# Layer 1 of a four-layer graph network: a node tile's transform made in two parts, the tile's own rows apart from its neighbours' sums

## The chip, the cores and the metric

The kernel runs on one core of one Trainium2 chip. The metric is the device time of one execution in microseconds (us), smaller is better. A core has five engines that run side by side, each in its own order: PE (TensorE, matrix products; its weight loads are shown as PEld), DVE (VectorE), ACT (ScalarE), POOL (GpSimd) and SP (SyncE, which only issues transfers), and 16 DMA engines that move data between the chip's memory (DRAM in the code) and the on-chip memories SBUF and PSUM. PE writes only to PSUM. A PSUM bank holds 128 rows of 512 numbers.

## What is computed

`x` is 6250 nodes of 256 numbers, `src` and `dst` name the ends of 100,000 edges, sorted by `dst`. The reference, cut:

```python
h = jnp.maximum(_layernorm(x, axis=-1), 0.0)
# in _L0_gnn_ref, features = h:
deg = jax.ops.segment_sum(jnp.ones(edge_dst.shape[0]), edge_dst, num_segments=n)
h = _sage_mean(features, edge_src, edge_dst, n, deg, W1_self, W1_neigh, b1)
h = _sage_pool(h, edge_src, edge_dst, n, deg, W2_pool, b2_pool, W2_self, W2_neigh, b2)
h = _sage_gcn(h, edge_src, edge_dst, n, deg, W3_neigh, b3)
h = _sage_mean(h, edge_src, edge_dst, n, deg, W4_self, W4_neigh, b4)
return x + (h @ W_fc + b_fc)

def _sage_mean(h, src, dst, n, deg, W_self, W_neigh, b):
    msum = jax.ops.segment_sum(h[src], dst, num_segments=n)
    h_neigh = msum / jnp.clip(deg, 1.0)[:, None]
    return h @ W_self + h_neigh @ W_neigh + b

def _sage_pool(h, src, dst, n, deg, W_pool, b_pool, W_self, W_neigh, b):
    hp = jax.nn.relu(h @ W_pool + b_pool)
    hmax = jax.ops.segment_max(hp[src], dst, num_segments=n)
    hmax = jnp.where(deg[:, None] > 0, hmax, 0.0)
    return h @ W_self + hmax @ W_neigh + b
```

The end nodes are not spread evenly: `dst` is 6250 times the square of a uniform number, so low nodes have many edges and high ones few.

## The kernel before, in words

Nodes lie in 49 tiles of 128 rows. Edges lie in 782 tiles of 128, in groups of four (G = 4). The first 8 node tiles of layer 1 are "hubs" (H1): for them a dense matrix of edge counts is built and multiplied. The other 41 tiles get their sums by gathers.

Layer 1 produces for each node tile the row that layer 2's pooling needs, `relu(h1 @ W_pool + b_pool)`, where h1 is layer 1's result. Because no nonlinearity stands between, `W1_self @ W2_pool` and `W1_neigh @ W2_pool` are multiplied out beforehand into `Wa` and `Wb`, and the biases into `crow`. So a tile's row is relu(own rows @ `Wa` + mean of the neighbours @ `Wb` + `crow`). It is stored in the DRAM table `tab_p`, from which layer 2 gathers. The transposed own rows and means are stored in `tab_t`, which layer 2 loads again.

The loop of layer 1 is `sums` (line 355), 474 steps of one edge tile each:

- `gather(j)`: POOL issues an indirect DMA of 128 rows of `tab_h` into one of 14 slots of `ring` (L374). A slot comes free when PE has used it.
- `one_hot(j)`: DVE makes the matrix `hot` that sorts the edges to rows (L370).
- PE multiplies `hot` with the three parts of the gathered rows (high, middle and low bits) into the bank `pg` (L392), 3 matmuls a step.
- `hub.advance`: some of the hubs' work. A build is two ACT instructions (`ht` L298, `hs` L300), one of DVE (`hm` L302) and a matmul into `pb` (L308), with a copy to `A` (L312) now and then; a product is three matmuls into `pd` (L430). All builds of the first hub are listed ahead of the loop.
- `next(todo[0])`: one piece of the oldest node tile that is ready. `todo` is a queue of generators; each call runs to the next `yield`.

After every fourth step DVE adds `pg` into the sums `acc` of the tiles that this group can touch (L409, L411), and a tile whose last group this is goes to `todo` as `done1(d, acc)`. Hubs go there when their dense product ends.

`done1` has, before the change, four pieces: (1) degree, its reciprocal (L787 to L789) and the mean `m1` on ACT (L791); (2) on PE six matmuls with the identity that transpose the three parts of the own rows `Z1` and add them up (L797) and two transposes of `m1` (L800), all into one bank `pt_m`, a copy by ACT to `th` (L802) and its store to `tab_t` (L803); (3) the product with `Wa` into `pm_hp` (L807); (4) the product with `Wb` onto it (L810), the addition of `crow` by DVE (L813), Relu by ACT (L814) and the store to `tab_p` (L815). An f32 product with 512 columns stands in the trace as two records for each matmul. The pools `pst` (tag `pt`) and `psm` (tag `pm`) have one bank each here.

The order in which each engine runs its instructions is not the order of the code: a scheduler goes by the code's order as a priority, and by its own estimate of when operands and buffers are ready. What it fixed is called the compiled order below. At run time each engine keeps to its order and waits on semaphores. SP issues nearly all plain transfers of this stage, in its own fixed order.

Layer 2 begins with gathers from `tab_p` (L1111), and each needs all of that table, so none starts before the last store of layer 1.

Of the kernel before, what the change touches and what calls it, by code (L numbers as in the profile page):

```python
# [9 lines left out]
F32 = mybir.dt.float32  # L10
# [4 lines left out]
AF = mybir.ActivationFunctionType  # L15
# [5 lines left out]
P = 128  # L21
# [51 lines left out]
def fast_path(  # L73
# [15 lines left out]
    nc = tc.nc  # L89
    N, FI = x.shape  # L90
    E = src.shape[0]
    FH = W1_self.shape[1]
    FO = W_fc.shape[1]
    NT = (N + P - 1) // P
    NFULL = N // P
    NREM = N - NFULL * P
    NP = NT * P
    T = (E + P - 1) // P
    EP = T * P
    KI = FI // P  # L100
# [9 lines left out]
    for d in range(NT):  # L110
        m, s = _edges_below(d * P, E, N)
        m1, s1 = _edges_below((d + 1) * P, E, N)
# [3 lines left out]
    JC = g_of[HUB[0]][0] * G // P  # L116
# [5 lines left out]
    for d in range(NT):  # L122
        m, s = _edges_below(d * P, E, N)
        m1, s1 = _edges_below((d + 1) * P, E, N)
# [7 lines left out]
    H1, H3, H4 = HUB  # L132
# [7 lines left out]
    for w0, w1_ in ((0, WT * H1), (WT * H1, NW)):  # L140
        for k in range(k_of[w0]):
            n = sum(1 for w in range(w0, w1_) if k_of[w] > k)
# [9 lines left out]
    dram = ctx.enter_context(tc.tile_pool(name="fdram", bufs=1, space=DRAM))  # L152

    tab_h = dram.tile([NP, 3 * FI], BF16, name="tab_h")
    tab_t = dram.tile([NT, P, FH], F32, name="tab_t")
    tab_p = dram.tile([NP, FH], F32, name="tab_p")
    tab_r = dram.tile([NP, 3 * FH], BF16, name="tab_r")
    tab_s = dram.tile([NP, 3 * FO], BF16, name="tab_s")
    tab_a = dram.tile([H4, P, NT, P // 2], BF16, name="tab_a")
# [27 lines left out]
    ident = const.tile([P, P], F32, name="identf")  # L187
    make_identity(nc, ident)
    ident_b = const.tile([P, P], BF16, name="ident_b")
# [30 lines left out]
    def bank(pool, tag, name, shape=None, bufs=None):  # L220
        t = pool.tile([P, FH], F32, tag=tag, name=name, **({"bufs": bufs} if bufs else {}))
        if shape is None:
            return t
        n = math.prod(shape)
        if len(shape) == 1:
            return t[:, :n]
        return t[:, :n].rearrange("p (a b) -> p a b", b=shape[1])
# [124 lines left out]
                self.done += 1  # L352


    def sums(pool, psg, table, F, srcT, keyT, jb, h, done, deep, hub, wait=0, counts=0, todo=()):

        ring = pool.tile([P, deep, 3 * F + 2 * counts], BF16, name="ring", bufs=1)  # L360
        if counts:
            nc.gpsimd.memset(ring[:, :, 3 * F :], 1.0)
        acc = {}
        ahead = 6
        hot = {}
        j0 = g_of[h][0] * G

        def one_hot(j):
            hot[j] = pool.tile([P, P], BF16, name="hot", bufs=ahead + 4)
            nc.vector.tensor_scalar(hot[j], iota_b, keyT[:, j - jb : j - jb + 1], None,  # L370
                                    op0=ALU.is_equal)

        def gather(j):
            nc.gpsimd.indirect_dma_start(  # L374
                out=ring[:, j % deep, : 3 * F], out_offset=None, in_=table,
                in_offset=bass.IndirectOffsetOnAxis(ap=srcT[:, j - jb : j - jb + 1], axis=0),
            )

        for j in range(j0, j0 + ahead):
            one_hot(j)  # L380
        for g in range(g_of[h][0], NG):
            pg = bank(psg, "pg", "pg", (F + counts,))
            n = min(G, T - g * G)
            for k in range(n):
                j = g * G + k
                X = ring[:, j % deep, :]
                gather(j)
                if j + ahead < T:
                    one_hot(j + ahead)
                for part in (2, 0, 1):  # L390
                    c = counts if part == 2 else 0
                    nc.tensor.matmul(  # L392
                        pg[:, : F + c], hot[j], X[:, part * F : (part + 1) * F + c],
                        start=(k == 0 and part == 2), stop=(k == n - 1 and part == 1),
                    )
                del hot[j]
                at = j - j0 + 1
                if at > wait:
                    hub.advance(math.ceil(len(hub.work) * (at - wait) / (T - j0 - wait)))
                if todo and next(todo[0], None) is None:  # L400
                    todo.pop(0)
            for d in range(h, NT):
                g0, g1 = g_of[d]
                if not g0 <= g <= g1:
                    continue
                m = M[:, m_at[d] + g - g0 : m_at[d] + g - g0 + 1]
                if d not in acc:
                    acc[d] = pool.tile([P, F + counts], F32, name="acc", bufs=3)
                    nc.vector.tensor_scalar(acc[d], pg, m, None, op0=ALU.mult)  # L409
                else:  # L410
                    nc.vector.scalar_tensor_tensor(acc[d], pg, m, acc[d],  # L411
                                                   op0=ALU.mult, op1=ALU.add)
                if g == g1:
                    todo.append(done(d, acc.pop(d)))
        while todo:
            for _ in todo.pop(0):
                pass
# [66 lines left out]
    Z1 = zpool.tile([P, NT, 3 * FI + 2], BF16, name="Z1")  # L484
# [8 lines left out]
    Wa = w1pool.tile([P, KI, FH], F32, name="Wa")  # L493
    Wb = w1pool.tile([P, KI, FH], F32, name="Wb")
    crow = w1pool.tile([P, FH], F32, name="crow")
    srcT = w1pool.tile([P, (JR - JC) * P], I32, name="srcT")
    keyT = w1pool.tile([P, (JR - JC) * P], F32, name="keyT")
# [4 lines left out]
    with ExitStack() as pro:  # L502
# [104 lines left out]
        i = 0  # L607
# [166 lines left out]
    with ExitStack() as on:  # L774
        pst = on.enter_context(tc.tile_pool(name="pst1", bufs=1, space=PSUM))
        psm = on.enter_context(tc.tile_pool(name="psm1", bufs=1, space=PSUM))
        psg = on.enter_context(tc.tile_pool(name="psg1", bufs=2, space=PSUM))
        psb = on.enter_context(tc.tile_pool(name="psb1", bufs=2, space=PSUM))
        psd = on.enter_context(tc.tile_pool(name="psd1", bufs=2, space=PSUM))
        wk = on.enter_context(tc.tile_pool(name="fl1", bufs=2))  # L780

        def h0_row(s):
            return Z1[:, s, :]

        def done1(d, acc):
            r = rmean[:, d : d + 1]
            nc.vector.tensor_copy(deg[:, d : d + 1], acc[:, FI : FI + 1])  # L787
            nc.vector.tensor_scalar_max(r, acc[:, FI : FI + 1], 1.0)
            nc.vector.reciprocal(r, r)  # L789
            m1 = wk.tile([P, FI], F32, name="m1")  # L790
            nc.scalar.activation(m1, acc[:, :FI], AF.Copy, scale=r)  # L791
            yield 1
            pt = bank(pst, "pt", "pt_m", (2 * KI, P))
            for k in range(KI):
                for part in range(3):
                    c = part * FI + k * P
                    nc.tensor.matmul(pt[:, k, :], Z1[:, d, c : c + P], ident_b,  # L797
                                     start=(part == 0), stop=(part == 2))
            for k in range(KI):
                nc.tensor.transpose(pt[:, KI + k, :], m1[:, k * P : (k + 1) * P], ident)  # L800
            th = wk.tile([P, 2 * KI, P], F32, name="th")
            nc.scalar.copy(th, pt)  # L802
            nc.sync.dma_start(tab_t[d].rearrange("p (k n) -> p k n", n=P), th)  # L803
            yield 1
            ph = bank(psm, "pm", "pm_hp")
            for k in range(KI):
                nc.tensor.matmul(ph, th[:, k, :], Wa[:, k, :], start=(k == 0), stop=False)  # L807
            yield 1
            for k in range(KI):
                nc.tensor.matmul(ph, th[:, KI + k, :], Wb[:, k, :], start=False,  # L810
                                 stop=(k == KI - 1))
            hp = wk.tile([P, FH], F32, name="hpf")
            nc.vector.tensor_add(hp, ph, crow)  # L813
            nc.scalar.activation(hp, hp, AF.Relu)  # L814
            nc.sync.dma_start(tab_p[d * P : (d + 1) * P, :], hp)  # L815

        As = [wk.tile([P, NT, P], F8, name=f"A{i}", bufs=1) for i in range(2)]
        keys = (sk1, mk1, 0)
        todo = []
        builds = [build(d, As[d % 2], keys, wk, psb) for d in range(H1)]  # L820
        denses = [dense(range(NT), lambda s, A=As[d % 2]: A[:, s, :], h0_row, FI, psd,
                        lambda acc, d=d: todo.append(done1(d, acc)), extra=1)
                  for d in range(H1)]
        work = list(builds[0])
        first = len(work)
        for d in range(H1):
            work += merged(denses[d], builds[d + 1]) if d + 1 < H1 else denses[d]
        hub = Hub(work)
        hub.advance(first)
        todo.append(segments())  # L830
        sums(wk, psg, tab_h, FI, srcT, keyT, JC * P, H1, done1, 14, hub, counts=1, todo=todo)
    layer1.close()


# [62 lines left out]
    jb = g_of[H3][0] * G  # L897
# [1029 lines left out]
```

## Time and profile before

| | |
|---|---|
| median of 18 runs | 3542.53 us (3525.9 to 3566.07) |
| the profiled execution | 3548.44 us |
| its span, first to last instruction | 3546.6 us |
| mean granted clock of PE | 0.872 of full speed |
| busy share PE, DVE, ACT, POOL | 73%, 55%, 25%, 58% |
| layer 1's loop, first gather to first gather of `tab_p` | 148.7 to 1055.4 us |

The span in 40 equal slices, as the page shows it, each digit tenths of a slice:

```profile
PE   2457777778876745676676767679689889688887
...
POOL 5363555455437676677766765550366666566663
PEclk9767888889898877788897888889899999899999
DMA  6443454445449999999999999991699999766664
```

Layer 1 is about slices 2 to 12. Layer 2, slices 13 to 28, is the stretch in which the DMA engines are full. Then come layers 3 and 4.

The columns of a group of instructions are: line, engine, operation, what it writes and reads, count, then busy time in us and mean ns of one, then the engine's idle time just before them and what ended it. A row of windows gives, for a stretch A:B in us, its length, each engine's busy time with its number of instructions, the granted clock, the share of the DMA engines and GB/s. A wait is put down to what came last by the profile.

### The profile page before, as it was taken

What the parts mean: (1) busy time and instruction counts of PE and PEld (TensorE: products, weight loads), DVE (VectorE), ACT (ScalarE), POOL (GpSimd) and SP (SyncE); (2) the same over time, 40 slices, a digit from 0 to 9 for tenths busy, and PEclk for the clock granted to TensorE, in tenths of its full rate; (3) what the DMA queues carried; (4) which work ended last, traced back from release to release, by engine and by line L of the source; (5) the groups of instructions that cost most, each with busy time, mean ns of one, the idle gap of its engine ahead of it and who ended that gap; (6) DMA issues with size and microseconds to landing.
All of it is one profiled execution on the core that took longest, in us unless ns stands there. A gap on an engine that the chain in (4) does not pass through costs nothing. (4 is left out here: it accounts for less than half of the span.)

```text
span 3546.6 us, 41171 instructions
## 1 busy us (share of the span) xinstructions
PE 2597.7 (73%) x12699; PEld 1437.3 (41%) x12699; DVE 1953.6 (55%) x5075; ACT 903.4 (25%) x2383; POOL 2040.6 (58%) x2260
## 2 busy tenths in 40 slices
PE   2457777778876745676676767679689889688887
PEld 1134444455544322232232323234233333477776
DVE  4744444444426767665665655553266566466664
ACT  2556555444414556621111111100000001000000
POOL 5363555455437676677766765550366666566663
PEclk9767888889898877788897888889899999899999
DMA  6443454445449999999999999991699999766664
GB/s 188 147 127 111 143 151 140 142 149 155 145 145 396 365 353 367 352 389 376 376 337 335 381 364 323 332 319 53 254 331 363 360 360 336 242 187 188 187 193 139
DMA packets 403406, 913.34 MB, mean 258 GB/s; under 512 B 58064, under 2 KB 151202, under 8 KB 403144
## 3 DMA queue, kind: packets, MB, share of 16 engines
q0 software_dynamic: 146560, 514.74, 44.1%
q1 hardware_dynamic: 198532, 340.44, 25.8%
q10 hardware_dynamic: 58084, 55.44, 5.0%
q8 instruction: 103, 1.69, 0.2%
q14 instruction: 127, 1.04, 0.1%
HBM read 610.65 MB, written 300.55 MB: 257 GB/s over the span
## 5 line engine op out<-in xcount | busy, mean ns | idle before, releaser
L1111 POOL DMA_INDIRECT X<-tab_p,srcIf x782 | 825.6, 1056 | 421.5 <-issue 204.5
L392 PE MATMUL pg<-ring,hot 128*128 128x256 bf16 (+2 forms) x3390 | 699.1, 315 | 131.4 <-DMA ring<-tab_r,srcE 51.5
L374 POOL DMA_INDIRECT ring<-tab_h,srcT x474 | 451.3, 952 | 427.0 <-PE pg L392 164.7
L430 PE MATMUL pd<-zt,ac 128*128 128x256 bf16 (+1 forms) x3462 | 581.5, 300 | 56.7 <-issue 41.3
L430 PE MATMUL pd<-r,ae 128*128 128x512 bf16 x1536 | 413.8, 421 | 211.6 <-DVE acc L908 100.0
L392 PEld LDWEIGHTS <-hot 128*128 128x128 bf16 x3390 | 336.9, 101 | 391.7 <-issue 222.4
L374 POOL DMA_INDIRECT ring<-tab_r,srcE x342 | 333.4, 975 | 190.4 <-PE pg L392 74.5
L1116 DVE SCALAR_TENSOR_TENSOR X<-X,samef,X 128x512 f32<-128x512 f32 x385 | 289.0, 751 | 270.3 <-DMA X<-tab_p,srcIf 137.2
L430 PEld LDWEIGHTS <-ac 128*128 128x128 fp8e4 x3462 | 337.9, 98 | 205.0 <-issue 78.7
L411 DVE SCALAR_TENSOR_TENSOR acc<-pg,M,acc 128x257 f32<-128x257 f32 (+2 forms) x518 | 274.5, 560 | 248.1 <-PE pg L392 204.3
L374 POOL DMA_INDIRECT ring<-tab_s,srcE x314 | 298.8, 952 | 190.8 <-issue 66.3
L308 PE MATMUL pb<-hm,hs 128*128 128x392 bf16 x781 | 266.0, 389 | 160.5 <-ACT A L312 36.1
L300 ACT ACTIVATE hs<-ht,onef 128x128 bf16<-128x128 bf16 x781 | 291.0, 395 | 361.4 <-PE pb L308 198.6
L1116 DVE SCALAR_TENSOR_TENSOR X<-X,samef 128x512 f32<-128x512 f32 x391 | 293.3, 751 | 145.0 <-DMA X<-tab_p,srcIf 113.0
L430 PEld LDWEIGHTS <-ae 128*128 128x128 fp8e4 x1536 | 162.7, 106 | 470.9 <-issue 346.6
L370 DVE TENSOR_SCALAR hot<-iota_bf,keyE 128x128 bf16<-128x128 bf16 x656 | 154.0, 268 | 166.7 <-PE pg L392 107.7
L1050 PE MATMUL pm_prf<-unf,hTf 128*128 128x512 f32 x392 | 208.3, 658 | 30.8 <-ACT hTf L1041 18.2
L302 DVE TENSOR_SCALAR hm<-iota_w,mk 128x392 bf16<-128x392 f16 x461 | 155.3, 345 | 133.4 <-PE pb L308 65.0
L370 DVE TENSOR_SCALAR hot<-iota_bf,keyT 128x128 bf16<-128x128 bf16 x474 | 126.2, 277 | 150.8 <-PE pb L308 55.4
L312 ACT ACTIVATE A<-pb 128x392 fp8e4<-128x392 f32 x288 | 140.2, 491 | 262.3 <-PE pb L308 134.0
L430 PE MATMUL pd<-Z,A 128*128 128x256 bf16 (+1 forms) x1176 | 197.5, 283 | 2.4 <-issue 1.7
L1183 DVE TENSOR_SCALAR_CACHE_REDUCE many<-ac 128x896 bf16<-128x896 fp8e4 (+2 forms) x144 | 139.0, 965 | 88.7 <-DMA ac<-tab_a 69.2
(273 smaller groups left out, 2805.6 us busy)
## 6 DMA issues: line engine op xcount, KB each, us to landing
runb<-X SPq DMA_DIRECT2D x391, 512.0 KB
tab_r<-r SPq DMA_DIRECT2D x49, 384.0 KB
tab_a<-A SPq DMA_DIRECT2D x18, 784.0 KB
tab_t<-th SPq DMA_DIRECT2D x49, 256.0 KB
tab_p<-hpf SPq DMA_DIRECT2D x49, 256.0 KB
th<-tab_t ACTq DMA_DIRECT2D x49, 256.0 KB
X<-tab_p,srcIf POOLq DMA_INDIRECT x782
ac<-tab_a ACTq DMA_DIRECT2D x108, 112.0 KB
```

What stands on the lines that cost most here:

```text
L300: nc.scalar.activation(hots[0], t, AF.Relu, bias=one, scale=-1.0)
L302: nc.vector.tensor_scalar(hots[1], iota_w, mk[:, r : r + 1], None, op0=ALU.is_equal)
L308: nc.tensor.matmul(hold[0], hots[0], hots[1], start=(k == 0), stop=(k == k_of[w] - 1))
L312: nc.scalar.copy(A[:, :, c : c + WIN], hold[0].rearrange("p (s c) -> p s c", c=WIN), saturate=True)
L370: nc.vector.tensor_scalar(hot[j], iota_b, keyT[:, j - jb : j - jb + 1], None, op0=ALU.is_equal)
L374: nc.gpsimd.indirect_dma_start(out=ring[:, j % deep, : 3 * F], out_offset=None, in_=table, in_offset=bass.IndirectOffsetOnAxis(ap=srcT[:, ...
L392: nc.tensor.matmul(pg[:, : F + c], hot[j], X[:, part * F : (part + 1) * F + c], start=(k == 0 and part == 2), stop=(k == n - 1 and part == 1),
L411: nc.vector.scalar_tensor_tensor(acc[d], pg, m, acc[d], op0=ALU.mult, op1=ALU.add)
L430: nc.tensor.matmul(hold[0][:, : F + c], a, z[:, part * F : (part + 1) * F + c], start=(s == ss[0] and part == 2), stop=(s == ss[-1] and pa ...
L1050: nc.tensor.matmul(pm, hT[:, c, :], un[:, c, :], start=False, stop=(c == KH - 1))
L1111: nc.gpsimd.indirect_dma_start(out=X[:, k, :], out_offset=None, in_=tab_p, in_offset=bass.IndirectOffsetOnAxis(ap=srcI[:, t : t + 1], axis=0),
L1116: nc.vector.scalar_tensor_tensor(X[:, k, :], prev, same[:, t : t + 1], X[:, k, :], op0=ALU.mult, op1=ALU.max,)
```

## The change

The node tile's transform becomes two generators. `own1(d)` transposes the own rows, stores them to `tab_t`, three steps later multiplies them with `Wa`, adds `crow` and stores the f32 row to a new DRAM table `tab_g`. The loop takes one piece of it in every step, through a new argument `beside`, from its first step on: the tiles 8 to 48 in order, and after each third of them a hub. `done1` loads the row from `tab_g` in its first piece, transposes only `m1` three steps later, multiplies with `Wb` three steps after that, and adds the loaded row in place of `crow`. It has seven pieces in place of four. `own1` uses the same two banks, and `tab_t` of a tile is written by two transfers.

```diff
+    tab_g = dram.tile([NP, FH], F32, name="tab_g")
...
-    def sums(pool, psg, table, F, srcT, keyT, jb, h, done, deep, hub, wait=0, counts=0, todo=()):
+    def sums(pool, psg, table, F, srcT, keyT, jb, h, done, deep, hub, wait=0, counts=0, todo=(),
+             beside=iter(())):
...
+                next(beside, None)
                 if todo and next(todo[0], None) is None:
                     todo.pop(0)
...
+        def own1(d):
+            pt = bank(pst, "pt", "pt_h", (KI, P))
+            for k in range(KI):
+                for part in range(3):
+                    c = part * FI + k * P
+                    nc.tensor.matmul(pt[:, k, :], Z1[:, d, c : c + P], ident_b,
+                                     start=(part == 0), stop=(part == 2))
+            hT = wk.tile([P, KI, P], F32, name="h0T")
+            nc.scalar.copy(hT, pt)
+            nc.sync.dma_start(tab_t[d, :, : KI * P].rearrange("p (k n) -> p k n", n=P), hT)
+            yield 1
+            yield 1
+            yield 1
+            pm = bank(psm, "pm", "pm_g")
+            for k in range(KI):
+                nc.tensor.matmul(pm, hT[:, k, :], Wa[:, k, :], start=(k == 0),
+                                 stop=(k == KI - 1))
+            g = wk.tile([P, FH], F32, name="grow")
+            nc.vector.tensor_add(g, pm, crow)
+            nc.sync.dma_start(tab_g[d * P : (d + 1) * P, :], g)
+            yield 1
...
         def done1(d, acc):
...
             nc.scalar.activation(m1, acc[:, :FI], AF.Copy, scale=r)
+            g = wk.tile([P, FH], F32, name="grow2")
+            nc.sync.dma_start(g, tab_g[d * P : (d + 1) * P, :])
             yield 1
-            pt = bank(pst, "pt", "pt_m", (2 * KI, P))
+            yield 1
+            yield 1
+            pt = bank(pst, "pt", "pt_m", (KI, P))
             for k in range(KI):
-                for part in range(3):
-                    c = part * FI + k * P
-                    nc.tensor.matmul(pt[:, k, :], Z1[:, d, c : c + P], ident_b,
-                                     start=(part == 0), stop=(part == 2))
-            for k in range(KI):
-                nc.tensor.transpose(pt[:, KI + k, :], m1[:, k * P : (k + 1) * P], ident)
-            th = wk.tile([P, 2 * KI, P], F32, name="th")
+                nc.tensor.transpose(pt[:, k, :], m1[:, k * P : (k + 1) * P], ident)
+            th = wk.tile([P, KI, P], F32, name="th")
             nc.scalar.copy(th, pt)
-            nc.sync.dma_start(tab_t[d].rearrange("p (k n) -> p k n", n=P), th)
+            nc.sync.dma_start(tab_t[d, :, KI * P :].rearrange("p (k n) -> p k n", n=P), th)
+            yield 1
+            yield 1
             yield 1
             ph = bank(psm, "pm", "pm_hp")
             for k in range(KI):
-                nc.tensor.matmul(ph, th[:, k, :], Wa[:, k, :], start=(k == 0), stop=False)
-            yield 1
-            for k in range(KI):
-                nc.tensor.matmul(ph, th[:, KI + k, :], Wb[:, k, :], start=False,
+                nc.tensor.matmul(ph, th[:, k, :], Wb[:, k, :], start=(k == 0),
                                  stop=(k == KI - 1))
-            hp = wk.tile([P, FH], F32, name="hpf")
-            nc.vector.tensor_add(hp, ph, crow)
-            nc.scalar.activation(hp, hp, AF.Relu)
-            nc.sync.dma_start(tab_p[d * P : (d + 1) * P, :], hp)
+            nc.vector.tensor_add(g, ph, g)
+            nc.scalar.activation(g, g, AF.Relu)
+            nc.sync.dma_start(tab_p[d * P : (d + 1) * P, :], g)
...
+        def owns():
+            hubs = list(range(H1))
+            for i, d in enumerate(range(H1, NT)):
+                yield from own1(d)
+                if i % 3 == 2 and hubs:
+                    yield from own1(hubs.pop(0))
+            for d in hubs:
+                yield from own1(d)
...
-        sums(wk, psg, tab_h, FI, srcT, keyT, JC * P, H1, done1, 14, hub, counts=1, todo=todo)
+        sums(wk, psg, tab_h, FI, srcT, keyT, JC * P, H1, done1, 14, hub, counts=1, todo=todo, beside=owns())
```

## The prediction

> **What bounds the kernel now.** The change touches layer 1 alone; in the compiled order of the changed kernel every engine's instructions from the first gather of `tab_p` on stand as before. So I read layer 1: first the waits of PE between 160 and 1060 us, then the stretches, one tile close up, and the gathers.
>
> The waits of PE (line, waited for: us in total, times, longest):
>
> ```profile
> PE pt_m L800 <- ACT m L791: 43.7, 14, 7.6
> PE pm_hp L807 <- ACT th L802: 39.4, 23, 3.8
> PE pt_m L800 <- issue: 20.8, 11, 3.2
> ...
> PE pt_m L800 <- ACT hs L300: 14.1, 4, 6.4
> ```
>
> All rows of `pt_m` L800 and `pm_hp` L807 together are 143 us: in a node tile PE stands before the transposes of `m1`, and again before the product, one step after the copy to `th`. One such tile, in order of time (start, length, engine, line):
>
> ```profile
> 612.84 0.57 PE L797 MATMUL pt_m<-ident_b,Z 128*128 128x128 bf16 x6
> ...
> 613.82 0.87 DVE L411 SCALAR_TENSOR_TENSOR acc<-pg,M,acc 128x257 f32<-128x257 f32 x2
> ...
> 616.32 0.49 ACT L791 ACTIVATE m<-acc,rmeanf 128x256 f32<-128x256 f32 x1
> ...
> 616.86 0.53 PE L800 MATMUL pt_m<-identf,m 128*128 128x128 f32 x2 [3.23 <-ACT m L791]
> ```
>
> The same stretch as windows (length, PE, PEld, DVE, ACT, POOL busy, granted clock, DMA share, GB/s):
>
> ```profile
> 604.80:613.60 8.80, 8.80 (x76) 6.80 (x73) 5.07 (x16) 4.62 (x13) 5.15 (x6) 1.00 0.57 167
> 613.60:616.80 3.20, 0.03 (x1) 0.00 (x0) 2.45 (x12) 3.10 (x9) 2.46 (x3) 1.00 0.39 111
> 616.80:623.90 7.10, 5.12 (x14) 2.65 (x15) 1.09 (x6) 1.87 (x5) 2.84 (x3) 0.52 0.50 153
> ```
>
> An idle of 3.2 us is followed by 7.1 us at half clock, so a stall costs about 3.2 + 3.4 us. Layer 1 in six stretches, same columns; the cuts are the first matmuls of steps 64, 90 and 196 (counted by the three `ring` matmuls of a step) and the end of step 473:
>
> ```profile
> 148.50:248.90 100.40, 50.15 (x253) 30.25 (x254) 40.35 (x157) 41.06 (x133) 67.35 (x71) 0.69 0.48 136
> 248.90:294.30 45.40, 27.57 (x75) 8.03 (x73) 22.07 (x72) 39.79 (x131) 7.13 (x8) 0.53 0.17 54
> 294.30:334.20 39.90, 29.64 (x159) 18.30 (x158) 14.71 (x55) 14.89 (x42) 22.91 (x24) 0.88 0.52 157
> 334.20:521.20 187.00, 142.19 (x821) 91.64 (x820) 85.07 (x301) 96.12 (x263) 101.03 (x106) 0.84 0.48 140
> 521.20:1038.50 517.30, 424.03 (x2481) 272.32 (x2479) 216.83 (x769) 228.74 (x581) 252.85 (x266) 0.88 0.49 147
> 1038.50:1055.40 16.90, 9.63 (x41) 4.62 (x38) 2.92 (x24) 3.82 (x7) 0.01 (x1) 0.96 0.35 122
> ```
>
> I call them Start, Block (the builds of the first hub, without gathers), S, B, C and Tail. In C a step takes 517.3 / 277 = 1.87 us and every other engine is under half busy: PE's work, its stalls and the half clock behind them set the pace. POOL waits for ring slots that PE frees late:
>
> ```profile
> POOL ring L374 <- PE pg L392: 164.7, 85, 35.5
> POOL ring L374 <- PE pb L308: 124.4, 89, 4.7
> ```
>
> A gather that waits for nothing takes 0.95 us and a 0.30 us gap, 1.255 in all; in Start, where PE is idle half the time, POOL makes 71 in 100.4 us, 1.41 each. That is the next bound.
>
> **PE's work at full clock.** A 256-column matmul costs 0.109 us (nine `pd` in 0.98 us on the chain of waits); a `pb` of 392 columns 0.167 by columns. From the last tile's timeline (L807 at 1047.39, L810 at 1049.21; L797 at 1045.22, L800 at 1045.55): one half of the product 1.82 or 1.72 us (four records), six Z transposes 0.33, the pair of `m1` 0.24 to 0.34. A tile is 4.1 us today; its own part (Z transposes and `Wa`) 2.1, its neighbours' part 2.0. Work in S: 78 `pg`, 24 `pd`, 9 `pb`, 3 tiles, 25 us. B: 318, 261, 104, 9 tiles, 117 us. C: 831, 885, 205, 35 tiles, 365 us.
>
> **The change, part by part.** PE's instructions stay 49 x 4.1 us; they move. In the compiled order the own parts do not run behind the first gathers: h0T's ACT copies stand behind all builds of the first hub, so one own part comes at step 64, 21 in S, 26 in B, one in C.
>
> - Block: 67 builds stand in one piece instead of 59; 45.4 / 60 = 0.76 us each, **+6 us** (bounds 0 and +10).
> - S: 25 - 3 x 2.1 + 21 x 2.1 = 63 us of work. All use one `pt` and one `pm` bank: the next `pm_g` waits for the DVE addition (0.69 us, the row of L813, and two hand-overs), while PE has the next transposes (0.33) and four `pg` (0.44). No row shows this pairing; below, no wait, 63; above, half clock throughout, 124. I take 0.6 us for each own part, 75: **+35 us** (+23 to +84).
> - B: 117 - 9 x 2.1 + 26 x 2.1 = 153 us of work; gathers alone 106 x 1.255 = 133, so PE still bounds. Above: today's 45 us of idle and clock of 0.84 remain, 153 / 0.84 + 45 = 227. With three steps between the pieces most stalls go; I take 165, nearer the work: **-22 us** (-34 to +40).
> - C: 365 - 35 x 2.1 = 292 us of work, under the gathers. `pt_m` stands two steps later behind the end of its group than today (step 124 against 122 for one tile), some 2.5 us or more against a mean stall of 2.8 (92.5 us in 33 waits), and `pm_hp` three steps behind `th` instead of one. POOL is up to 14 steps ahead at step 196, so 263 gathers set the end: at 1.255 us 330, at Start's 1.41 371. I take 1.45, for the waits on DVE and `hs` that stay, and 4 us to land: 385, **-132 us**. Below 350; above, today's 93 us of idle and 62 of lost clock stay, 292 + 155 = 447 (-167 to -70).
> - Tail: three neighbours' parts (6 us of PE) stand where two whole tiles (8) stood: **-2 us** (-5 to 0).
> - Cover. DVE gets 49 additions of 0.69, 34 us on 382 busy of 907; ACT 49 more copies (two of 256 columns by the 0.475 us of `m1` from `pd`, against 0.586: +18 us on 424). Both lie beside PE. DMA: 49 stores and 49 loads of 256 KB, 25.7 MB on 133 MB, share 0.48 to about 0.57. SP issues 147 more DMAs, 0.32 us each; POOL gets none. SP is passed in order: the load of `grow2` can wait there behind a store of `tab_t`, `tab_p` or `tab_a` whose producer is late, and `tab_p` of the same tile and the next loads stand behind it. It has six steps (over 7 us) before the addition needs it; a store of this size takes 2.8 us from issue to landing (`tab_p` issued 1052.57, the gather released 1055.38). Uncovered it would hold the `pm` bank, so PE, 2.8 us in each of 49 tiles, 137 us.
>
> Sum: 6 + 35 - 22 - 132 - 2 = **-115 us**; all bounds together -183 to +64. The profiled span 3546.6 becomes 3432, with the 1.8 us around it 3433; the median of the runs lies 5.9 us under that execution, so **3428 us**.
>
> One rule of the Trainium skill speaks against C. The row: in Start PE is half idle in pieces and the granted clock is 0.69. The page TensorE: Matmul & The Clock Gate, section "A second HAM failure mode: psum-queue depth-cycling", says that frequent short idles between groups of matmuls suffice to make the clock swing. By that rule PE, waiting a little for each gather, would stay throttled and C's work would be 292 / 0.69 = 423 us, the first rival.
>
> **The rivals.**
> 1. C's waits change their cause but not their size: PE, now waiting for gathers, keeps a low granted clock, as in Start, or `hs` and `acc` stall it. For it: Start's clock; waits on DVE and `hs` are already in the list. Against it: idles must last some 3 us to show a drop, and C's gathers come every 1.3 us. C at 445: 3428 + 60 = **3488 us**.
> 2. Slower: the own parts on single `pt` and `pm` banks. Each `pm_g` waits for an h0T copy that stands in ACT's order among the builds, and each wait drops the clock. Price as today's: 143 us / 49 = 2.9 us idle a tile and two thirds more in clock (62 to 93 us in C), 4.9 us for 47 tiles in S and B: 63 + 153 + 230 = 446 instead of 240, **3634 us**. It decides from about 115 / 47 = 2.4 us over my price for each own part. Against it: ACT is under half busy in B and the pieces stand three steps apart there; in S they stand close, which speaks for it.
> 3. The change does not do what it says: own parts pile up in S and B and C's gain is lost there or to the load of `grow2`: **3543 us**.
>
> **How the numbers follow.** Forecast 0.58, rival 1 0.25, rival 2 0.12, rival 3 0.05. The forecast's own range is 3390 to 3475; to hold 8 in 10 the range takes in rival 1 and ends at 3530; below, C at its floor with S as taken gives 3393, and a little less with B at its work, 3380. A measurement of this kernel tells about 0.2% (7 us) from no change. Faster: 0.58 + 0.25 = 0.83; same 0.04; slower 0.13, rival 2 and a part of 3.
>
> **What would show it.** Right: PE's waits at `pt_m` and `pm_hp` fall from 143 to under 40 us; step 90 comes later (about 375 against 334), step 196 at about 540, step 473 at about 925, the first gather of `tab_p` near 940; in C the gap before most gathers is 0.30 <-issue and the clock near 1.0. Wrong: a clock under 0.85 in C (rival 1), or `pm_g` waiting for ACT h0T or DVE `grow` over 2 us a tile and step 196 after 620 (rival 2).

## The result, and the profile after

The changed kernel takes 3458.25 us, the median of 10 runs (3433.0 to 3466.25), against 3545.23 us of the kernel before over all its runs beside it: a ratio of 0.9748 [0.973, 0.9767]. Run again later (e9 below) it took 3457.2 us against 3546.68, 0.9749 [0.9702, 0.9796]. It is faster, and inside the range; the forecast of 3428 us was 30 us too low. The profiled span falls from 3546.6 to 3461.2 us, by 85 us, and all of it is in layer 1: 906.9 to 821.1 us. What follows the first gather of `tab_p` takes 2492.1 us against 2491.3.

The six stretches of the changed kernel, cut at the same steps as before (length, PE, PEld, DVE, ACT, POOL busy, granted clock, DMA share, GB/s):

```profile
148.00:250.10 102.10, 51.89 (x257) 30.04 (x257) 41.46 (x155) 43.27 (x140) 68.12 (x72) 0.70 0.47 135
250.10:302.80 52.70, 32.56 (x87) 9.65 (x86) 23.98 (x76) 45.68 (x152) 6.43 (x7) 0.54 0.15 48
302.80:372.60 69.80, 67.27 (x344) 35.45 (x342) 30.33 (x79) 22.06 (x61) 23.76 (x25) 1.00 0.70 226
372.60:543.30 170.70, 158.04 (x1003) 102.84 (x1001) 98.36 (x328) 104.72 (x290) 101.71 (x107) 0.99 0.73 224
543.30:951.20 407.90, 329.15 (x2119) 228.01 (x2118) 203.36 (x764) 214.07 (x576) 252.21 (x264) 0.91 0.64 194
951.20:969.10 17.90, 9.12 (x30) 3.96 (x28) 4.48 (x26) 4.30 (x9) 0.02 (x1) 0.96 0.55 172
```

| stretch | before | after | difference | predicted |
|---|---|---|---|---|
| Start | 100.4 | 102.1 | +2 | 0 |
| Block | 45.4 | 52.7 | +7 | +6 |
| S, steps 64 to 90 | 39.9 | 69.8 | +30 | +35 |
| B, steps 90 to 196 | 187.0 | 170.7 | -16 | -22 |
| C, steps 196 to 473 | 517.3 | 407.9 | -109 | -132 |
| Tail | 16.9 | 17.9 | +1 | -2 |
| sum | 906.9 | 821.1 | -86 | -115 |

In S and B PE is busy for 96% and 93% of the time, at full clock: the own parts fill what were stalls. Of the 29 us that are missing, 23 are in C. There PE has 292 us of work by the prediction's count and needs 329 us for it at a clock of 0.91, and stands for another 79 us. Its waits in C (line, waited for: us in total, times, longest; L825 are the transposes of `m1`, L834 the product with `Wb`):

```profile
PE pd L433 <- issue: 10.5, 10, 3.1
PE pm_hp L834 <- issue: 9.9, 5, 3.8
PE pt_m L825 <- DMA ring<-tab_h,srcT: 8.8, 4, 3.4
PE pt_m L825 <- ACT hs L301: 8.8, 2, 4.8
PE pm_hp L834 <- ACT th L827: 7.8, 5, 3.2
PE pt_m L825 <- ACT m L817: 6.7, 5, 2.1
```

All rows of these two places in C make 53 us, where they were 89 before (L800 and L807). So the waits there have become fewer, not rare, and none of PE's waits here is at a `pg` for its gather. The instruction that waits is certain in these rows; the name behind the arrow is less so, as this trace holds only a part of the signals between engines (in C 237 of ACT's 563 and 250 of DVE's 619). The new waits of the own parts, in S and B, are small, 13.7 us in all (L794 the own transposes, L804 the product with `Wa`; the longest three):

```profile
PE pt_h L794 <- ACT th L827: 5.3, 4, 3.0
PE pm_g L804 <- DVE grow L836: 4.4, 2, 3.9
PE pm_g L804 <- DVE grow L807: 1.8, 2, 1.4
```

And the load of `grow2`, which the prediction had hidden behind six steps, is waited for by DVE twice in 49 tiles:

```profile
DVE grow L836 <- DMA grow<-tab_g: 6.5, 2, 4.0
```

### The profile page after: what moved, and what is told of

The parts are those of the page before. It is cut to its first block, busy times and chain, and to the rows that moved or that the text cites. A ratio compares the mean times of both kernels' runs of the same rounds, so it can differ in the third digit from the quotient of the medians.

```text
span 3461.2 us, 41603 instructions
## 1 busy us (share of the span) xinstructions
PE 2567.9 (74%) x12699; PEld 1421.1 (41%) x12699; DVE 1968.9 (57%) x5124; ACT 906.2 (26%) x2432; POOL 2032.3 (59%) x2260
## 5 line engine op out<-in xcount | busy, mean ns | idle before, releaser
L1145 POOL DMA_INDIRECT X<-tab_p,srcIf x782 | 816.8, 1044 | 437.8 <-issue 237.4
L433 PE MATMUL pd<-r,ae 128*128 128x512 bf16 x1536 | 420.8, 426 | 222.0 <-DVE acc L942 105.8
L1150 DVE SCALAR_TENSOR_TENSOR X<-X,samef 128x512 f32<-128x512 f32 x391 | 293.2, 751 | 161.8 <-DMA X<-tab_p,srcIf 120.0
```

The costliest lines, as they stand in the source:

```text
L433: nc.tensor.matmul(hold[0][:, : F + c], a, z[:, part * F : (part + 1) * F + c], start=(s == ss[0] and part == 2), stop=(s == ss[-1] and pa ...
L1145: nc.gpsimd.indirect_dma_start(out=X[:, k, :], out_offset=None, in_=tab_p, in_offset=bass.IndirectOffsetOnAxis(ap=srcI[:, t : t + 1], axis=0),
L1150: nc.vector.scalar_tensor_tensor(X[:, k, :], prev, same[:, t : t + 1], X[:, k, :], op0=ALU.mult, op1=ALU.max,)
```

## The experiments

What had to be told apart: whether the gain is owed to the split or to the three steps between the pieces; why C ends at 408 us and not at 385; and whether the 59 us of own parts in S and B, and the block of builds in front of them, are a price that can be avoided.

The runs fell on several chips of the same type. On two of them (e1 to e4; e9 and e10) the kernel before takes 3554.65 and 3546.68 us, as on the chip of the prediction; on two others (e5 to e8; e11 and e12) it takes 3201.33 and 3203.04 us. I call them the 3550 chips and the 3200 chips. Each of these four was used for one set of runs only, so whether the kind belongs to the chip or to that hour isn't known. A ratio is always to the kernel before on the same chip.

| kernel | chip | us | ratio |
|---|---|---|---|
| e1, steps alone | 3550 | 3444.28 | 0.9714 [0.9661, 0.9766] |
| e2, split alone | 3550 | 3503.4 | 0.9868 [0.9817, 0.992] |
| e3, mean on DVE | 3550 | 3471.28 | 0.9781 [0.9733, 0.983] |
| e4, own parts among the builds | 3550 | 3428.14 | 0.9658 [0.9611, 0.9706] |
| e5, the change with six steps | 3200 | 3228.61 | 1.0093 [1.0076, 1.011] |
| e6, six steps alone | 3200 | 3206.98 | 1.0003 [0.9973, 1.0034] |
| e7, e4 with six steps | 3200 | 3200.45 | 0.9997 [0.9979, 1.0015] |
| e8, e4, own parts in every second step | 3200 | 3169.04 | 0.9914 [0.989, 0.9937] |
| e9, the change again | 3550 | 3457.2 | 0.9749 [0.9702, 0.9796] |
| e10, the kernel of e8 | 3550 | 3402.71 | 0.9579 [0.953, 0.9628] |
| e11, the kernel of e5 | 3200 | 3223.99 | 1.0075 [1.005, 1.0099] |
| e12, e8 with six steps | 3200 | 3159.8 | 0.9875 [0.9835, 0.9915] |

### e1: the steps without the split

The kernel before, with three steps between the pieces of `done1` and the two halves of the product in one piece:

```diff
             nc.scalar.activation(m1, acc[:, :FI], AF.Copy, scale=r)
             yield 1
+            yield 1
+            yield 1
             pt = bank(pst, "pt", "pt_m", (2 * KI, P))
...
             yield 1
+            yield 1
+            yield 1
             ph = bank(psm, "pm", "pm_hp")
...
-            yield 1
```

> The kernel before, with three steps between done1's pieces and nothing split: own rows, Wa and the single tab_t store stay in done1, no tab_g. Theory 1 (PE is the bound nearly everywhere in layer 1, the gain is the stalls taken away, and moving own work from C to S and B is a wash): C = 365 us of work + the 79 us idle and 37 us of lost clock that the changed kernel keeps there = 481 (before 517), B near its gathers, 150 (before 187), S and Block as before; about -75 us, 3465 us. Theory 2 (the split is what pays, because it moves 73 us of PE work out of C): less than half of the gain, 3500 to 3540 us.

Measured 3444.28 us, 0.9714 [0.9661, 0.9766]; layer 1 takes 804.5 us. S, B, C and Tail:

```profile
292.80:326.40 33.60, 27.97 (x151) 17.35 (x149) 12.62 (x46) 11.97 (x34) 18.81 (x20) 0.88 0.53 158
326.40:496.80 170.40, 136.43 (x829) 89.25 (x827) 81.82 (x309) 97.30 (x271) 106.08 (x112) 0.91 0.55 160
496.80:929.00 432.20, 378.59 (x2457) 257.69 (x2456) 203.22 (x768) 222.82 (x579) 252.03 (x265) 0.96 0.58 174
929.00:953.20 24.20, 17.00 (x64) 7.94 (x61) 4.25 (x25) 4.83 (x9) 0.00 (x0) 1.00 0.33 118
```

The steps alone bring all of the gain: C falls by 85 us with every tile's 4.1 us of work still in it, and the clock there rises from 0.88 to 0.96. Set against this kernel, the changed one saves 24 us in C and 6 in Tail and pays 47 in Start, Block and S; 16.6 us more in sum, the 821.1 against 804.5. The intervals of the two ratios overlap, so neither a loss by the split nor a gain of a few us is shown here; e5 and e6, which differ in the split alone, show a loss on the other kind of chip.

### e2: the split without the steps

The changed kernel with the neighbours' pieces one step apart:

```diff
             yield 1
-            yield 1
-            yield 1
             pt = bank(pst, "pt", "pt_m", (KI, P))
...
             yield 1
-            yield 1
-            yield 1
             ph = bank(psm, "pm", "pm_hp")
```

> The changed kernel with one step between done1's pieces, as before the change; own1 and tab_g stay. Theory 1: the stalls are back, C = 292 of work + 93 idle + 62 clock = 447 (-70 against before), B = 153 + 70 = 223 (+36), S 78 (+38), Block +7: about 3545 to 3560 us, no faster than before. Theory 2: most of the gain stays, 3460 to 3490 us.

Measured 3503.4 us, 0.9868 [0.9817, 0.992]. B and C:

```profile
375.20:552.60 177.40, 162.96 (x1002) 103.66 (x1001) 97.36 (x326) 103.38 (x288) 100.46 (x106) 0.97 0.71 214
552.60:1001.80 449.20, 340.50 (x2129) 228.97 (x2128) 208.69 (x770) 217.35 (x581) 250.90 (x265) 0.89 0.60 179
```

C comes out at 449 us, close to the 447 that the prediction had as its upper bound for stalls that stay. One step instead of three costs 41 us there. B, however, stays short at 177 us: there PE waits 13.6 us at the two places, 1.5 a tile, against 108 in C, 3.1 a tile. In B the steps hold own work as well, so more work of PE lies between the pieces. That fits a distance that is counted in PE's work between two pieces and not in steps; B and C differ in other work too, so it isn't shown by itself.

### e3: the mean on DVE

```diff
-            nc.scalar.activation(m1, acc[:, :FI], AF.Copy, scale=r)
+            nc.vector.tensor_scalar(m1, acc[:, :FI], r, None, op0=ALU.mult)
```

> The changed kernel with the mean m1 made by DVE (a multiplication by the column r) in place of ACT. Theory 3 (the chain to pt_m is long because m1 stands in ACT's order among the builds, and acc, which m1 frees, is what stops the gathers at step 64): the waits at pt_m in C fall from 30 to under 15 us, and the Block (52 us, 67 builds in one piece) dissolves, as the compiled order has the gathers run on; 3385 to 3425 us. Rival: the builds and own parts that leave Block and S pile up in B (48 own parts there) and only a few us are won, 3435 to 3460 us.

Measured 3471.28 us, 0.9781 [0.9733, 0.983]. S, B and C:

```profile
250.20:289.00 38.80, 22.32 (x103) 12.37 (x104) 16.02 (x64) 15.81 (x52) 25.70 (x27) 0.63 0.50 139
289.00:552.90 263.90, 240.01 (x1323) 137.57 (x1322) 136.68 (x433) 153.21 (x441) 105.82 (x111) 0.93 0.62 193
552.90:958.00 405.10, 327.27 (x2120) 223.85 (x2119) 213.57 (x799) 204.01 (x541) 252.19 (x264) 0.92 0.66 195
```

With the mean off ACT's queue the waits at `pt_m` in C fall from 29.5 to 13.3 us, and those at `pm_hp` (30, from 23) and `pd` (23, from 16) take their place: C is 405 us. That is far from the 3385 to 3425 us of the first theory and above its rival too. The compiled order of the whole stage moves with this one instruction, too: the block of builds is gone (5.6 us), and the builds and own parts pile up in B, which takes 264 us. Taking this one operand out of ACT's queue didn't shorten C.

### e4: own parts among the builds

The builds of the first hub no longer stand in one piece ahead of the loop; after every second one comes a piece of an own part:

```diff
-        hub.advance(first)
...
+        beside = owns()
+        for k in range(first):
+            hub.advance(k + 1)
+            if k % 2:
+                next(beside, None)
```

> The changed kernel with one piece of own1 after each second build of the first hub, ahead of the loop, so that 18 own parts lie in Start, 21 in S and 10 in B of the compiled order (1, 21 and 26 before). If PE's idle half of Start is free for them: B falls from 171 to near its gathers, 150, Start stays near 102: 3435 to 3445 us. Rival: Start gets longer by what B loses, because the h0T copies stand in ACT's order ahead of builds and on one pt bank: 3450 to 3470 us.

Measured 3428.14 us, 0.9658 [0.9611, 0.9706]; layer 1 takes 785.3 us. Start, Block and C:

```profile
148.70:253.10 104.40, 78.16 (x439) 42.45 (x438) 57.36 (x206) 71.92 (x239) 67.93 (x72) 0.91 0.64 188
253.10:276.00 22.90, 17.15 (x71) 7.44 (x70) 12.66 (x43) 19.98 (x66) 6.80 (x7) 0.93 0.47 148
506.70:916.10 409.40, 329.71 (x2120) 227.95 (x2118) 205.22 (x772) 215.98 (x583) 254.54 (x268) 0.92 0.65 195
```

This does what the words of the change say and the change itself didn't: work runs behind the first gathers. Start holds 26 us more of PE's time in about the same length, and the block shrinks from 52.7 to 22.9 us. B, where the gain was expected, falls only from 170.7 to 161.8. C stays where it was.

### e5, e6 and e7: six steps instead of three

If C's residual waits come from too short a distance, more distance takes them away. The two oldest tiles go forward in each step, with six steps between the pieces (in the changed kernel for e5, in e1's for e6, in e4's for e7):

```diff
-                if todo and next(todo[0], None) is None:
-                    todo.pop(0)
+                for t in todo[:near]:
+                    if next(t, None) is None:
+                        todo.remove(t)
...
             yield 1
+            yield 1
+            yield 1
+            yield 1
```

> The changed kernel with six steps instead of three between done1's pieces, and the two oldest tiles of the queue advanced in each step, so that a tile still takes 6.5 steps of the queue. Theory 1a (what C keeps, 52 us of waits at pt_m and pm_hp and the half clock behind them, is still distance that is too short once PE runs at 0.8 us a step): those waits fall under 15 us, C goes from 408 to 365 to 385 us, 3420 to 3440 us. Rival (as the mean on DVE hints: a wait that is taken away comes back at the next instruction, because PE is paced by ACT's and DVE's orders as a whole): C stays within 10 us of 408, 3450 to 3462 us.

> The same longer distance (six steps, two tiles at a time) without the split, on the kernel of the first experiment. Theory 1a: C = 365 us of work and some 40 of rest, 400 to 410 instead of 432, 3410 to 3425 us. Rival: C unchanged, 3440 to 3450 us. Theory 2 (the split pays once the waits are gone, as it moves 73 us of PE work out of C): this one stays over 25 us behind the same distance with the split.

> Own parts among the first builds (as in the fourth experiment, 3428 us) and six steps with two tiles at a time. If the two gains are of different stretches they add: C from 409 to 365 to 385, 3388 to 3405 us. If C is not set by the waits of pt_m and pm_hp: 3420 to 3430 us.

These ran on a 3200 chip: 3228.61 us (1.0093), 3206.98 (1.0003) and 3200.45 (0.9997). Against the kernel before on that chip nothing is won, and e5 loses 0.9%. S and C of e5, then S and C of e6, and what PE waits for in C of e6:

```profile
276.80:347.60 70.80, 67.15 (x345) 35.30 (x343) 30.07 (x79) 22.20 (x61) 23.62 (x25) 1.00 0.69 217
500.00:841.00 341.00, 303.90 (x2123) 219.71 (x2122) 208.28 (x765) 212.95 (x576) 251.06 (x265) 0.97 0.76 234
```

```profile
268.90:294.20 25.30, 24.82 (x152) 16.18 (x150) 14.09 (x56) 13.80 (x41) 14.66 (x16) 0.99 0.58 168
429.20:795.90 366.70, 361.56 (x2464) 254.53 (x2463) 207.29 (x768) 219.49 (x578) 259.57 (x273) 1.00 0.69 210
```

```profile
PE pg L392 <- DMA ring<-tab_h,srcT: 4.6, 4, 2.4
PE pd L431 <- ACT A L312: 0.4, 2, 0.2
```

Here the count of the prediction is to be seen by itself: C's work of 365 us takes 366.7 us with PE at full clock and 5 us of waits. The kernel before must be near this on such a chip. It has no profile there; its 3201.33 us less about 149 us ahead of the loop and 2384 after it (e6) leave some 668 us for layer 1, by this estimate as much as e6's 671.4. Where there are few stalls, the steps have nothing to take away. e5 differs from e6 by the split alone, on the same chip, and is 22 us slower, with intervals that lie apart. In the profiled executions layer 1 takes 710.4 us against 671.4: S, B and the block grow by 46, 17 and 8 us, and C and Tail give back 26 and 6 (what follows layer 1 was 16 us shorter in that execution of e5). So here the split is a loss, and the second theory written down for e6 fails. The changed kernel as it is was not run on a 3200 chip; e5 and e11 differ from it by the six steps.

### e8: own parts in every second step

The kernel of e4, with a piece of an own part in every second step of the loop:

```diff
-                next(beside, None)
+                if at % 2:
+                    next(beside, None)
```

> Own parts among the first builds, and in the loop a piece of own1 only in every second step: 10 own parts in S instead of 21, 13 in B, 8 in C, where the fourth experiment had none. If C has room that PE does not use (its rest of 79 us idle): S falls from 69 to about 48, C grows by less than 8, 3408 to 3418 us. If own work costs its 2.1 us wherever it stands: 3425 to 3435 us.

Measured 3169.04 us, 0.9914 [0.989, 0.9937], the best of this chip; layer 1 takes 640.1 us, S 43.3 instead of e7's 69.2. (e7 has six steps, too; e12 below, with six steps, has S at 43.2, so the shorter S comes from the spreading.) Its C, what PE waits for there, and the first rows of POOL's waits:

```profile
420.50:768.30 347.80, 315.98 (x2194) 225.38 (x2192) 213.53 (x776) 218.00 (x586) 260.46 (x274) 0.99 0.80 242
```

```profile
PE pg L394 <- DMA ring<-tab_h,srcT: 29.3, 42, 2.4
PE pg L394 <- DVE acc L415: 1.0, 2, 0.8
```

```profile
POOL ring L376 <- issue: 30.2, 99, 0.3
POOL ring L376 <- PE pg L394: 16.8, 55, 0.3
```

This is the picture that the prediction drew of C: PE waits for gathers and for hardly anything else (29.3 of 31.2 us), no gather waits longer than 0.3 us, and 274 of them take 347.8 us, 1.27 each. It is reached with three steps, not six.

### e9 and e10: the same kernels on a 3550 chip

The changed kernel, and the kernel of e8, without an edit.

> The changed kernel as it is, run again to learn how it stands on whichever chip this is. Theory 1 (the stall that the three steps take away is PE waiting for its half's chain, and the split only moves 59 us of work into S and the block before it): on a chip where the kernel before takes about 3545 us, 0.975 as measured. On a chip where the kernel before takes about 3201 us its layer 1 is short by the same stalls, C is near its 365 us of work already, and what is left is C down to about 310 to 340 (its work of 292 us and some waits) against S and the block up by some 40: ratio 0.985 to 1.005, about 3150 to 3215 us. Theory 2 (the gain is the same anywhere): 0.975, about 3121 us on such a chip.

> The kernel of e8 again, beside the changed kernel on the same chip. If the spreading of the own parts is worth what e4 showed on its own (36 us of layer 1 from the block alone), it is 30 to 50 us faster than the changed kernel on either kind of chip: ratio about 0.963 where the kernel before takes about 3545 us, 0.991 where it takes about 3201 us. If it is only the chip: no faster than the changed kernel.

Measured 0.9749 for the changed kernel, as the first time, and 3402.71 us, 0.9579 [0.953, 0.9628], for the kernel of e8, 54 us faster than the changed kernel beside it. (On the 3200 chip it was under 1% faster than the kernel before.) Against e4, which has three steps as well, layer 1 falls from 785.3 to 768.4 us: S gives 26 us, and B and C take some back. C of e10 and PE's longest waits in it (in this kernel L826 and L835 are the two places of the neighbours' part):

```profile
486.10:897.90 411.80, 341.74 (x2195) 234.23 (x2194) 210.36 (x776) 219.38 (x586) 251.32 (x265) 0.92 0.67 200
```

```profile
PE pm_hp L835 <- issue: 15.8, 7, 4.5
PE pt_m L826 <- ACT ht L299: 10.5, 5, 3.2
PE pt_m L826 <- ACT m L818: 8.1, 4, 2.6
PE pm_hp L835 <- ACT th L828: 5.4, 3, 4.0
```

The same program, the same order on each engine: 347.8 us with no wait at `pt_m` but one of 0.2 us, and here 411.8 us with the waits of the changed kernel back. So on a 3200 chip three steps are distance enough for the chain from `m1` to the product, and on a 3550 chip something in that chain is late. One such wait of e10 in order of time (start, length, engine, line; in brackets the idle time before it and what ended it):

```profile
755.48 0.49 PE L434 MATMUL pd<-Z,A 128*128 128x257 bf16 x3
...
756.27 0.40 ACT L299 ACTIVATE ht<-iota_bf,sk 128x128 bf16<-128x128 bf16 x1
...
759.71 0.32 DVE L303 TENSOR_SCALAR hm<-iota_w,mk 128x392 bf16<-128x392 f16 x1 [2.31 <-remote]
759.71 0.40 ACT L301 ACTIVATE hs<-ht,onef 128x128 bf16<-128x128 bf16 x1 [3.04 <-remote]
...
760.02 0.35 ACT L828 COPY th<-pt_m 128x256 f32<-128x256 f32 x1
760.04 0.98 POOL L376 DMA_INDIRECT ring<-tab_h,srcT  x1 [1.51 <-remote]
...
760.43 2.93 PE L835 MATMUL pm_hp<-Wb,th 128*128 128x512 f32 x3 [4.45 <-issue]
```

PE stops at 755.97 in front of a product whose operand `th` is not copied yet. The copy stands in ACT's queue behind an `hs`, and ACT stands in front of that `hs` for 3.04 us. DVE starts in the same hundredth of a microsecond and POOL 0.33 us later, after waits of the same kind. The view says "remote" because it finds no instruction that ends close to the signal. The trace does tell whose signal it is: all three wait for the semaphore that PE's matmuls raise, and six of its records stand between 759.69 and 759.99, when PE had begun no matmul since 755.70. So PE waits for `th`, the copy for ACT's queue, and ACT for PE's own signal of a matmul that by the records was long over.

That is the difference between the two kinds of chip. In C of e8 each of 597 signals of PE is recorded within 0.02 us of the end of a matmul; in C of e10 132 of 535 come over 1 us after the last such end, up to 5.2 us. The changed kernel has 168 of 548, the kernel before 105 of 547. All eight traces of 3550 chips show it in C and none of the six of 3200 chips, and the signals of DVE and ACT are within 0.04 us in both. The ends of matmuls are modelled in the profile, so it stays open whether the matmuls end later there or only their signal does, and why.

### e11 and e12: more distance, again

The kernel of e5, and the kernel of e8 with the edit of e5.

> The changed kernel with six steps between the pieces of the neighbours' part and two tiles under way, as e5. On a chip where the kernel before takes about 3545 us, where the changed kernel itself takes 3458: theory 1 (what is left of waits in C is the half's own chain, m1 to the turn and th to the product, still late because three steps of PE work pass in a few us) has C fall from 407 to 340 to 365 and the waits at pt_m and pm_hp in C from 52 us to under 20: 0.957 to 0.965, about 3400 to 3420 us. Theory 2 (a rate that the chip itself sets holds C at 264 gathers in 400 us or more, or PE stops for something that all engines share, and the waits only change their names): C stays at 395 to 410 and the time at 0.972 to 0.978. On a chip where the kernel before takes about 3201 us this is e5 again, 1.009.

> The kernel of e8 and e10 (own parts among the first hub's builds, then in every second step) with six steps between the pieces and two tiles under way. Theory 1: on a chip where the kernel before takes about 3545 us, C falls from 412 to 345 to 370 and the time from 0.958 to 0.940 to 0.950, 3330 to 3370 us. Theory 2: C stays at 400 or more, 0.955 to 0.962. On a chip where the kernel before takes about 3201 us, where C of e8 took 348: 0.986 to 0.993.

Both fell on a 3200 chip again: 3223.99 us, 1.0075 [1.005, 1.0099], and 3159.8 us, 0.9875 [0.9835, 0.9915]. C of e12:

```profile
420.80:768.10 347.30, 317.38 (x2199) 227.57 (x2197) 214.49 (x776) 216.32 (x586) 258.45 (x273) 0.98 0.79 243
```

347.3 us against e8's 347.8: beyond three steps the distance changes nothing there, and the interval overlaps that of e8. Whether six steps would cover the late signals on a 3550 chip was to be told by these two runs and is not: it was not tried there.

## Why the prediction was right, and where not

- The bound. Right for the chip it was made on. PE's stalls and the half clock behind them set C's pace: the steps alone (e1) take 85 us out of C without taking any work out.
- Which part brings it. The prediction priced the split and the steps together in C and let the split's 73 us (35 own parts of 2.1) fall into the gain. By e1 the split gains nothing that shows in the time, and by e5 against e6 it loses 22 us on a 3200 chip: its work comes back in S and in the block, and in C its place is taken by stalls and a lower clock (in the changed kernel PE stands 79 us and its work takes 37 us longer than counted; in e1 it stands 54 us, at a clock of 0.96).
- Block, S, B. The block grew by 7 us for 6, S took 69.8 us for 75 and B 170.7 for 165. The 0.6 us for each own part in S was too much: 69.8 - 63 is 6.8 us for 21 of them, 0.32 each. The single banks cost PE 7.8 us of waits at `pm_g` and 5.9 at `pt_h` in S and B, for 47 tiles, so the second rival's 4.9 us a tile has no place; step 196 came at 543.3, where "after 620" was its sign.
- C, the term that was mis-sized. The step that failed is "I take 1.45, for the waits on DVE and `hs` that stay, and 4 us to land: 385". It measured 407.9 us, 1.54 us for each of the 263 gathers with the 4 us taken off, and PE wasn't waiting for them. What stands in its place in e10's records is PE's late signals, which hold up the gathers and ACT's queue with `m1` and `th` in it; the sum had no term for that. Both bounds were reached in other runs: the lower, 350, by e11's 338.0 and e8's 347.8 us on chips without the late signals, the upper, 447, by e2's 449.2 with the distance taken away. The signs show the same: the waits at `pt_m` and `pm_hp`, to fall under 40 us, are 53 in C alone; the clock is 0.91; step 473 comes at 951.2 for 925 and the first gather of `tab_p` at 969.1 for 940. C hardly moves in any later version on a 3550 chip with three steps and most own parts ahead of C: 405 to 412 us in e3, e4, e9 and e10.
- The first rival, C at 445 with a low clock, is not what happened, though C went 23 of the 60 us towards it. Its rule, that frequent short idles between groups of matmuls make the clock swing (the Trainium skill, TensorE: Matmul & The Clock Gate, section "A second HAM failure mode: psum-queue depth-cycling"), shows little in the run that fits it best: in C of e8 PE waits for gathers 42 times, 29.3 us in all and never over 2.4 us, and the clock is 0.99. Start, from which the rival took its 0.69, is another case: 41 of PE's 50 us of idle there lie in five waits of 5.8 to 13.0 us. Nor does an idle need the 3 us that the prediction held against this rival: in e8 a wait of 2.4 us is followed by 3.4 us at half clock.
- The cover of `grow2`. Right: 6.5 us of waits, where 137 was the price without cover. SP waits 26.7 us in front of these loads for stores of `tab_p`; DVE's 6.5 us are all that a load of `grow2` held up.
- Tail. +1 for -2; the difference is small and was not looked into.
- The sum. -86 for -115: 23 us of the 29 are C's size, 6 are B, 3 the Tail, 2 Start, 1 Block, and S gave 5 back (rounded one by one).

## What to carry to other kernels

When PE stands before an operand that another engine makes, first try to move the use some work away; that is a few lines, and on the 3550 chips it brought the whole gain of this change; on a 3200 chip, where the operand came in time, there was none to bring. Moving PE's work out of a stretch pays only if the stretch it goes to has idle time of its own: in S it cost nearly its full length, between the builds (e4) it took idle time instead. Look in the compiled order at where moved work lands: "behind the first gathers" became true only when the code put the pieces between the builds.

## What the runs showed of the hardware

- The same kernel takes 3546.68 us on one chip and 3201.33 on another, nearly 10% less, and the worth of an edit changes with it: e8's kernel stands at 0.9579 and at 0.9914.
- PE's signals tell the two kinds apart: of those recorded in C, 132 of 535 come over 1 us behind the last end of a matmul in e10, and none of 597 over 0.02 us in e8.
- The pace of the gathers follows it. Counted from the starts of POOL's gathers in C, the median distance is 1.25 us on both. In e8 and e12 no gather comes more than 2 us after the one before it. In e10 54 of them do, 128.2 us together, so 128.2 - 54 x 1.255 = 60 us more than at the common pace, close to the 64 us by which the two C differ; in the changed kernel it is the same, 54 and 128.3 us. They mostly come every four to six gathers. Each of the 54 waits for PE's signal that a slot is free, and 49 of them start within 0.25 us after a record of it (48 in the changed kernel), though by PE's records the slot had been free for some 4 us in the median and POOL was some 10 gathers ahead of PE. The transfers are not slower, as far as their packets show: with each gather's packets counted off in order of time, the last ends 3.1 us after the issue in C of e10 and 3.5 us in C of e8 (medians).
- In Start the gathers came every 1.41 us in the kernel before, and every 1.25 us on the 3200 chips. So the 1.41 that the prediction used as the slower of its two gather paces was no price of the kernel but of the chip.
